# Denser stops, split comparisons and a moved gather in a two-layer graph kernel (quantile aggregation, then message passing) on one core

## The chip, the cores and the metric

The kernel runs on one core of a Trainium2 chip. The metric is the device time of one execution in microseconds (us); lower is better. TensorE is called PE here, its weight loads PEld, VectorE DVE, ScalarE ACT, GpSimd POOL, and SyncE, which issues most of the DMAs, SP.

## The reference, cut to what matters

Sixteen batches of 1,024 nodes with 64 features each, and a symmetric 0/1 adjacency with self-loops, about 16 neighbours to a node. Every node counts as present (`nodemask` is all ones).

```python
# layer 0
nb      = (adj > 0) & ~eye;  m = nb.sum(-1);  rank = cumsum(nb, -1) - 1
skip    = where(m > 10, (m + 1) // 2, 1)
removed = nb & (skip > 1) & ((rank + 1) % skip == 0)
valid   = where(removed | removed.T, 0, adj) > 0          # thinned neighbours, self included
sv      = sort(where(valid, x[None, :, :], big), axis=neighbours)   # for every node and feature
agg     = sum(wt * quantile(sv, tau) for tau, wt in ((.25, .25), (.5, .5), (.75, .25)))
x       = layernorm(x + relu((x + agg) @ W1 + b1) @ W2 + b2)
# layer 1
msg     = adj @ x
x       = layernorm(x + tanh(concat(x, msg) @ W1 + b1) @ W2 + b2)
```

The quantiles interpolate linearly between two places of the sorted list, as is usual. The edge part of layer 1 does not reach the output.

## The kernel before, in words

The 16 batches are treated in nine groups, of 1, 2, 2, 2, 2, 2, 2, 2 and 1 batches. A group goes through these stages, and neighbouring groups overlap.

**Find** (per batch). The adjacency is loaded (`a`, L509, by SP), turned into signs (`nb`, L517), transposed on PE (`nb_t`, L545 and L549), and the neighbours are ranked by products with triangular blocks (`p_rank`, L593 and L596, taken out by ACT as `gone`, L598). What remains is `valid` (L618 to L625). The nodes are sorted by their number of neighbours and put in that order by products with a permutation (`p_srt`, L687 to L691); then DVE reads the neighbours' numbers out of packed words (`codes`, `listed`). The result is `group.index`, the row in `x` of every neighbour of every node.

**Gather**. The sorted nodes of a group make 8·G tiles of 128 nodes (G is 1 or 2), taken in pairs. For every neighbour slot of a tile, POOL issues one indirect DMA (L876) that brings 128 rows of 64 float32 values into the cell `g[:, j]`. Four buffers `g0` to `g3` (`RING = 4`) hold one pair each. A group of two batches has 230 such gathers, its eight pairs 43, 36, 32, 29, 27, 24, 21 and 18; the program has 1,859. Because the nodes are sorted, the first tile has the longest lists. Its slots 24 to 34 are needed by few nodes (the table `FEW`: 23 nodes for slot 24, one for slot 34). In groups 1 to 8 these rare slots are not gathered one by one: 22 small DMAs on SP collect the indices into one column (`few<-index`, L885), ACT fills `few_x` (L886), one indirect DMA on POOL gets all the rows (L887), and 22 DMAs on SP carry them to their cells (`g<-few_x`, L892).

**Sort**. For each node and feature the list is brought into order as far as the quantiles need it, by a network of minima and maxima on DVE: 4,982 `tensor_tensor` instructions on `g` in all, each over 64 to 1,024 elements of a partition. Those of the two tiles of a pair are interleaved. After the last one of a tile, `weigh` lets ACT multiply the needed cells by the quantiles' weights (L907), in place; `add_up` adds them on PE with an identity (`p_agg`, L924 and L928), and ACT takes the sums out as `agg` (L936). A pair's buffer is then free for gathers to come.

**Close** (per batch). The sums go back to the nodes' own order (`p_g`, L965), through the MLP and the layernorm, and layer 1 follows with transposed adjacency blocks (`a_block`, `p_adj` L1135, `adj_t` L1137) and messages (`p_msg`, L1144). For the last groups some of the blocks are transposed ahead (`a_ahead`).

**The order.** The Python code writes the program in an order set by a clock of its own: all DVE instructions pass through the class `Counted`, whose `issue` adds up a modelled time `now` (their line in the profile is L443, whatever they do). `Steps` spreads the steps of find and close over that time: a step is written when its due time has come. The main loop writes the compares of a pair turn by turn, and `around` writes between them what is due. A framework then sets the waits and issues by readiness: the written order is a priority, and each engine's queue runs in order.

**The stops.** In `issue`, ahead of a DVE instruction with two tensor inputs, once `now` has reached `due`, a short one-input reduction is put in (`pause`, L437), which reads two values of the cell written four compares ago; `due` is then set to `GATHER = 1.32` us later. A one-input instruction that passes the due time counts as a stop itself.

```python
if two and self.now >= self.due and len(self.written) >= 4:
    nc.vector.tensor_reduce(pause, self.written[-4], AX.X, ALU.max)
    self.due = self.now + GATHER
```

Of the kernel before, what the change touches and what calls it, by code (L numbers as in the profile page):

```python
# [157 lines left out]
def kernel(  # L158
# [240 lines left out]
    GATHER = 1.32  # L399
# [8 lines left out]
    class Counted:  # L408
# [9 lines left out]
        def __getattr__(self, name):  # L418
# [6 lines left out]
            def issue(out, *args, **more):  # L425
# [10 lines left out]
                if two and self.now >= self.due and len(self.written) >= 4:  # L436
                    nc.vector.tensor_reduce(pause, self.written[-4], AX.X, ALU.max)  # L437
                    self.due = self.now + GATHER
                    self.now += 0.065
                elif not two and self.now + us >= self.due:  # L440
                    self.due = max(self.now, self.due) + GATHER
# [38 lines left out]
    class Group:  # L480


        def __init__(self, number, start, G):
# [3 lines left out]
            self.early = None  # L487
# [343 lines left out]
    def cells(g, box, which, width):  # L831

        start, (d1, n1), (d2, n2) = box
        return bass.AP(tensor=g.tensor, offset=g.offset + start[which] * width,
                       ap=[g.ap[0], [d2[which] * width, n2], [d1[which] * width, n1], [1, width]])
# [15 lines left out]
    def gather(group, at, sorts, lists):  # L851
# [20 lines left out]
        for k, part in zip(pair, parts):  # L872
            u, v = divmod(k, G)
            for j in range(1, min(FEW) if k == 0 and group.number > 0 else TILES[G][k][0]):
                slot_no = first[u] + j - 1
                nc.gpsimd.indirect_dma_start(  # L876
                    out=part[:, j, :], out_offset=None, in_=x_rows,
                    in_offset=bass.IndirectOffsetOnAxis(ap=group.index[:, v, slot_no:slot_no + 1], axis=0),
                    bounds_check=limit, oob_is_err=False)
        if at == 0 and group.number > 0:  # L880
            rows, many = slice(0, G * (P // 2)), lists.tile([P, 1], I32, name="few")
            got = lists.tile([P, C], F32, name="few_x")
            for there, here, j in few(G):
# [3 lines left out]
            nc.gpsimd.indirect_dma_start(  # L887
                out=got[rows], out_offset=None, in_=x_rows,
                in_offset=bass.IndirectOffsetOnAxis(ap=many[rows], axis=0),
                bounds_check=limit, oob_is_err=False)  # L890
            for there, here, j in few(G):
                nc.sync.dma_start(parts[0][here, j], got[there])  # L892
        return parts

    def sort(group, k, g):
# [5 lines left out]
        def compare(op, box):  # L901
            vector.tensor_tensor(cells(g, box, 2, C), cells(g, box, 0, C), cells(g, box, 1, C),
                                    op=op)
            vector.written = vector.written[-3:] + [g[:, box[0][2], :2]]
# [566 lines left out]
```

## Time and profile before

| what | value |
|---|---|
| three runs | 3887.37, 3934.4, 4052.67 us (median 3934.4) |
| the profiled execution | 3815.42 us, span 3813.7 us |
| mean granted TensorE clock in it | 0.709 |
| busy: DVE | 2329.5 us, 61% of the span |
| busy: POOL | 2104.7 us, 55% |
| busy: PE | 1942.5 us, 51% |
| busy: ACT | 1324.3 us, 35% |
| DMA | 205.67 MB, mean 54 GB/s |

The span runs from the first to the last recorded work of the execution; its own device time is 1.7 us longer. A busy share is an average over stages with different limits. In a row of instructions the columns are the line and engine, the operation with output and inputs, the count, the busy time in us and the mean of one in ns, and after the second bar the idle time of the engine just before these instructions, with what ended most of it. "remote" stands for a release that the profile puts down to no engine of this core, "issue" for time in which the engine waited for nothing that the profile shows. SPq is the DMA queue that SP issues to.

### The profile page before, as it was taken

To read this page: it belongs to the slowest core of one execution; us is meant where nothing else is said; L and a number is where in the kernel's file an instruction comes from. 1 tells how busy PE (TensorE), PEld (TensorE's weight loads), DVE (VectorE), ACT (ScalarE), POOL (GpSimd) and SP (SyncE) were. 2 spreads that over 40 slices of the span, in tenths; PEclk is the share of its full clock that TensorE was granted. 3 is DMA by queue.
4 is the path that set the end of the run, shared out by engine and by line. 5 is a ranking of instruction groups with operands and counts; after the bars stand their busy time and mean duration, and the time that the engine had idled before them with its cause. 6 is when DMAs were issued, how large, how long until landed. Compare 5 with 4: busy or idle time off the path is not lost.

```text
span 3813.7 us, 37663 instructions
## 1 busy us (share of the span) xinstructions
PE 1942.5 (51%) x10312; PEld 1070.0 (28%) x10312; DVE 2329.5 (61%) x9225; ACT 1324.3 (35%) x2945; POOL 2104.7 (55%) x1943
## 2 busy tenths in 40 slices
PE   5206523731565442963439635674336645674376
PEld 3103312420333221532224323332113323242133
DVE  4208624991598635885268844877248765768653
ACT  3204423431443332542325323544224334134123
POOL 1760346077654766167572677447571576757750
PEclk9556756765788666875669756786667866777578
DMA  2101111121212201222022212032021321242111
GB/s 99 20 19 48 58 50 32 65 52 24 64 44 87 66 18 62 82 66 43 17 67 93 67 30 65 23 105 64 18 66 28 94 58 26 60 117 62 20 47 29
DMA packets 268306, 205.67 MB, mean 54 GB/s; under 512 B 92634, under 2 KB 225290, under 8 KB 268086
## 3 DMA queue, kind: packets, MB, share of 16 engines
q1 hardware_dynamic: 207382, 147.10, 12.1%
q0 software_dynamic: 59744, 55.90, 7.5%
q8 instruction: 83, 1.36, 0.2%
q14 instruction: 137, 1.12, 0.1%
q10 hardware_dynamic: 960, 0.18, 0.0%
HBM read 203.97 MB, written 4.19 MB: 55 GB/s over the span
## 4 chain that ended last, share of the span: by engine, by line
PE 30%; another core or an unknown queue 25%; DVE 22%; ACT 9%; issue 8%; POOL 4%; DMA 1%; SPq 0%; ACTq 0%; DVEq 0%; POOLq 0%
DVE g L443 12%; PE p_msg L1144 5%; POOL g L876 4%; PE p_srt L687 3%; PE p_g L965 3%; PE p_adj L1135 2%; PE p_rank L596 2%; PE p_rank L593 2%; PE p_agg L924 2%; PE p_cnt L564 1%; PE p_nb L545 1%; ACT nb_t L549 1%; ACT g L907 1%; DVE codes L443 1%
## 5 line engine op out<-in xcount | busy, mean ns | idle before, releaser
L876 POOL DMA_INDIRECT g<-in_x_dram,index x1859 | 2075.7, 1117 | 1470.3 <-issue 560.1
L443 DVE TENSOR_TENSOR g<-g 128x128 f32<-128x128 f32 (+7 forms) x4982 | 1581.3, 373 | 199.7 <-remote 93.7
L545 PE MATMUL p_nb<-ident_h,nb 128*128 128x128 bf16 x1024 | 107.9, 280 | 649.6 <-DVE nb L443 261.9
L437 DVE TENSOR_REDUCE pause<-g 128x1 f32<-128x2 f32 x1021 | 148.5, 145 | 272.2 <-ACT g L907 240.5
L907 ACT ACTIVATE g<-g,weights 128x64 f32<-128x64 f32 x1006 | 260.0, 338 | 102.7 <-DVE g L443 84.3
L965 PE MATMUL p_g<-back,parts 128*64 128x512 bf16 x720 | 197.9, 425 | 186.6 <-DVE back L443 138.5
L443 DVE TENSOR_SCALAR gone<-gone,s 128x1024 bf16<-128x1024 f16 x128 | 64.3, 503 | 362.8 <-ACT gone L598 222.8
L598 ACT ACTIVATE gone<-p_rank,s 128x1024 f16<-128x1024 f32 x128 | 141.5, 1112 | 402.2 <-remote 303.2
L545 PEld LDWEIGHTS <-nb 128*128 128x128 bf16 x1024 | 92.6, 130 | 670.4 <-issue 489.9
L1144 PE MATMUL p_msg<-adj_t,x 128*64 128x512 f32 x416 | 232.3, 661 | 65.9 <-issue 30.4
L593 PE MATMUL p_rank<-after,blocks 8*128 8x512 bf16 x256 | 121.4, 474 | 282.0 <-ACT gone L598 147.5
L549 ACT ACTIVATE nb_t<-p_nb 128x1024 bf16<-128x1024 bf16 x124 | 122.1, 1023 | 375.0 <-remote 247.9
L924 PE MATMUL p_agg<-g,ident 128*128 128x128 f32 x918 | 161.6, 332 | 131.3 <-ACT g L907 83.7
L687 PE MATMUL p_srt<-pay,perm 128*128 128x323 bf16 x1024 | 187.0, 320 | 52.0 <-DVE x_q L443 29.4
L625 ACT ACTIVATE valid<-p_stay 128x1024 bf16<-128x1024 f32 x128 | 130.4, 1019 | 173.5 <-remote 95.0
L924 PEld LDWEIGHTS p_agg<-g,ident 128*128 128x128 f32 x918 | 143.0, 236 | 151.9 <-ACT g L907 96.4
L1137 ACT COPY adj_t<-p_adj 128x512 f32<-128x512 f32 x208 | 117.4, 584 | 162.6 <-PE p_adj L1135 79.0
L596 PEld LDWEIGHTS <-nb_t 128*128 128x128 bf16 x1024 | 70.6, 111 | 365.1 <-issue 365.1
L618 PE MATMUL p_stay<-nb,ident_h 128*128 128x512 bf16 x256 | 115.1, 450 | 105.8 <-ACT valid L625 56.3
L965 PEld LDWEIGHTS <-parts 128*64 128x64 bf16 x720 | 80.0, 119 | 280.1 <-issue 178.8
L517 ACT ACTIVATE nb<-a 128x1024 bf16<-128x1024 f32 x124 | 125.4, 1051 | 67.2 <-remote 27.1
L1135 PE MATMUL p_adj<-ident,a_block 128*128 128x128 f32 x832 | 138.6, 300 | 14.3 <-ACT z_t L1156 11.6
(188 smaller groups left out, 3054.9 us busy)
## 6 DMA issues: line engine op xcount, KB each, us to landing
a<-in_adj_dram SPq DMA_DIRECT2D x64, 1024.0 KB
a_block<-in_adj_dram SPq DMA_DIRECT2D x208, 256.0 KB
g<-in_x_dram,index POOLq DMA_INDIRECT x1859
a_ahead<-in_adj_dram SPq DMA_DIRECT2D x48, 256.0 KB
x_f<-in_x_dram SPq DMA_DIRECT2D x16, 256.0 KB
out_dram<-o SPq DMA_DIRECT2D x16, 256.0 KB
x_c<-in_x_dram SPq DMA_DIRECT2D x15, 256.0 KB
few<-index SPq DMA_DIRECT2D x45, 0.0 KB
```

What stands on the lines that cost most here:

```text
L437: nc.vector.tensor_reduce(pause, self.written[-4], AX.X, ALU.max)
L443: return getattr(nc.vector, name)(out, *args, **more)
L545: nc.tensor.transpose(p[:, t], v["nb"][:, t, block(j)], ident_h)
L549: nc.scalar.activation(v["nb_t"][:, j], p.rearrange("p t c -> p (t c)"), AF.Relu)
L593: nc.tensor.matmul(p[:, half_of(h)], v["blocks"][:, block(t)], after[:, half_of(h)], start=True, stop=False, skip_group_check=True)
L687: nc.tensor.matmul(p[:, k, :PAY], v["perm"][:, t, block(2 * at + k)], pay[:, t], start=(t == 0), stop=False, skip_group_check=True)
L876: nc.gpsimd.indirect_dma_start(out=part[:, j, :], out_offset=None, in_=x_rows, in_offset=bass.IndirectOffsetOnAxis(ap=group.index[:, v, sl ...
L907: nc.scalar.mul(g[:, cell], g[:, cell], group.weights[:, v, u, place:place + 1])
L924: nc.tensor.matmul(p, ident, it, start=(k == 0), stop=(k == most - 1), skip_group_check=True)
L965: nc.tensor.matmul(v["p_g"][h][:C, :HALF], v["parts"][:, k, q], m[:, half_of(h)], start=(k == 0 and v["start"]), stop=(k == 2 and q == v[" ...
L1135: nc.tensor.transpose(p[:, block(t)], m[:, t], ident)
L1144: nc.tensor.matmul(v["p_msg"][C:2 * C, :HALF], v["x1"][:, j, :], adj_t, start=(j == 0), stop=(j == NT - 1))
```

## The change

There are four edits.

1. `GATHER = 1.32` becomes `STOP = 0.44`: the stops are written at least 0.44 us of modelled time apart in place of 1.32. A stop needs only one entry in `written` (before: four), which now keeps eight, as pairs of list and cell; it still reads the fourth-last entry, or the oldest one if there are fewer.
2. `compare` may be cut along its 64 columns. A piece is to end at the due time of the next stop, rounded to an even number of columns; a cut is made only if both pieces have at least `SPLIT = 0.1` us.
3. `weigh` takes the entries of the list that is being weighed out of `written`.
4. The rare slots: the 22 index DMAs and ACT's fill are written ahead of the first tile's gathers, the one indirect DMA behind its 12th slot (`ask`), and the 22 carrying DMAs (`give`) are put off: they are written when the compares of the previous group's last pair begin, or at the latest when their own group's turn comes.

```diff
--- before.py
+++ after.py
@@ -396,7 +396,8 @@
     CLOSING, CLOSING_LAST = 0.8, 60.0
     TURNING = 40.0
     RING = 4
-    GATHER = 1.32
+    STOP = 0.44
+    SPLIT = 0.1
     pause = const.tile([P, 1], F32, name="pause")
 
     def block(t):
@@ -433,12 +434,13 @@
                 us = 0.067 + more_us + n * each
                 two = name in ("tensor_tensor", "tensor_add", "tensor_sub", "tensor_mul",
                                "scalar_tensor_tensor")
-                if two and self.now >= self.due and len(self.written) >= 4:
-                    nc.vector.tensor_reduce(pause, self.written[-4], AX.X, ALU.max)
-                    self.due = self.now + GATHER
+                if two and self.now >= self.due and self.written:
+                    g, cell = self.written[-4:][0]
+                    nc.vector.tensor_reduce(pause, g[:, cell, :2], AX.X, ALU.max)
+                    self.due = self.now + STOP
                     self.now += 0.065
                 elif not two and self.now + us >= self.due:
-                    self.due = max(self.now, self.due) + GATHER
+                    self.due = max(self.now, self.due) + STOP
                 self.now += us
                 return getattr(nc.vector, name)(out, *args, **more)
             return issue
@@ -484,7 +486,7 @@
             self.number, self.start, self.G = number, start, G
             self.x_q, self.node, self.agg = [None] * G, [None] * G, [None] * G
             self.turned = [{} if number >= len(sizes) - 2 else None for _ in range(G)]
-            self.early = None
+            self.early = self.give_few = None
             self.pairs = [(k, k + 1) for k in range(0, NT * G, 2)]
 
         def parts(self, i):
@@ -828,11 +830,12 @@
             to.add(0.2, weigh)
         return to
 
-    def cells(g, box, which, width):
+    def cells(g, box, which, width, columns):
 
         start, (d1, n1), (d2, n2) = box
-        return bass.AP(tensor=g.tensor, offset=g.offset + start[which] * width,
-                       ap=[g.ap[0], [d2[which] * width, n2], [d1[which] * width, n1], [1, width]])
+        return bass.AP(tensor=g.tensor, offset=g.offset + start[which] * width + columns.start,
+                       ap=[g.ap[0], [d2[which] * width, n2], [d1[which] * width, n1],
+                           [1, columns.stop - columns.start]])
 
     def few(G):
 
@@ -869,27 +872,40 @@
                     if which == v:
                         nc.scalar.copy(part[here, 0], group.x_q[i][here, u])
         filled[at % RING] = max(filled[at % RING], start)
-        for k, part in zip(pair, parts):
-            u, v = divmod(k, G)
-            for j in range(1, min(FEW) if k == 0 and group.number > 0 else TILES[G][k][0]):
-                slot_no = first[u] + j - 1
-                nc.gpsimd.indirect_dma_start(
-                    out=part[:, j, :], out_offset=None, in_=x_rows,
-                    in_offset=bass.IndirectOffsetOnAxis(ap=group.index[:, v, slot_no:slot_no + 1], axis=0),
-                    bounds_check=limit, oob_is_err=False)
-        if at == 0 and group.number > 0:
+        rare = at == 0 and group.number > 0
+
+        def few_of_them():
             rows, many = slice(0, G * (P // 2)), lists.tile([P, 1], I32, name="few")
             got = lists.tile([P, C], F32, name="few_x")
             for there, here, j in few(G):
                 slot_no = first[0] + j - 1
                 nc.sync.dma_start(many[there], group.index[here, 0, slot_no:slot_no + 1])
             nc.scalar.copy(got, few_fill.to_broadcast([P, C]))
-            nc.gpsimd.indirect_dma_start(
-                out=got[rows], out_offset=None, in_=x_rows,
-                in_offset=bass.IndirectOffsetOnAxis(ap=many[rows], axis=0),
-                bounds_check=limit, oob_is_err=False)
-            for there, here, j in few(G):
-                nc.sync.dma_start(parts[0][here, j], got[there])
+
+            def ask():
+                nc.gpsimd.indirect_dma_start(
+                    out=got[rows], out_offset=None, in_=x_rows,
+                    in_offset=bass.IndirectOffsetOnAxis(ap=many[rows], axis=0),
+                    bounds_check=limit, oob_is_err=False)
+
+            def give():
+                for there, here, j in few(G):
+                    nc.sync.dma_start(parts[0][here, j], got[there])
+
+            return ask, give
+
+        if rare:
+            ask, group.give_few = few_of_them()
+        for k, part in zip(pair, parts):
+            u, v = divmod(k, G)
+            for j in range(1, min(FEW) if rare and k == 0 else TILES[G][k][0]):
+                slot_no = first[u] + j - 1
+                nc.gpsimd.indirect_dma_start(
+                    out=part[:, j, :], out_offset=None, in_=x_rows,
+                    in_offset=bass.IndirectOffsetOnAxis(ap=group.index[:, v, slot_no:slot_no + 1], axis=0),
+                    bounds_check=limit, oob_is_err=False)
+                if rare and k == 0 and j == min(FEW) // 2:
+                    ask()
         return parts
 
     def sort(group, k, g):
@@ -899,11 +915,21 @@
         todo = []
 
         def compare(op, box):
-            vector.tensor_tensor(cells(g, box, 2, C), cells(g, box, 0, C), cells(g, box, 1, C),
-                                    op=op)
-            vector.written = vector.written[-3:] + [g[:, box[0][2], :2]]
+
+            us = 0.00104 * C * box[1][1] * box[2][1]
+            done = 0
+            while done < C:
+
+                due = vector.due if vector.now < vector.due else vector.now + 0.065 + STOP
+                many = 2 * int(C * (due - vector.now - 0.067) / us / 2 + 0.5)
+                to = C if many * us / C < SPLIT or (C - done - many) * us / C < SPLIT else done + many
+                vector.tensor_tensor(*[cells(g, box, which, C, slice(done, to)) for which in (2, 0, 1)],
+                                     op=op)
+                done = to
+            vector.written = vector.written[-7:] + [(g, box[0][2])]
 
         def weigh(cell, place):
+            vector.written = [w for w in vector.written if w[0] is not g]
             nc.scalar.mul(g[:, cell], g[:, cell], group.weights[:, v, u, place:place + 1])
 
         for op, box in steps:
@@ -1259,11 +1285,19 @@
                 asked[group.number, at] = gather(group, at, sorts, lists)
                 room -= 1
 
+        def give_few(group):
+            if group.give_few:
+                group.give_few()
+                group.give_few = None
+
         for group in groups:
             while group.number not in found:
                 around(group.number - 1, True)
+            give_few(group)
             for at, pair in enumerate(group.pairs):
                 around(group.number)
+                if at == len(group.pairs) - 1 and group is not groups[-1]:
+                    give_few(groups[group.number + 1])
                 lists_of = [sort(group, k, g) for k, g in zip(pair, asked[group.number, at])]
                 turns = sorted(((n + 0.5) / len(l), k, n) for k, (l, _) in enumerate(lists_of)
                                for n in range(len(l)))
```

## The prediction, made before the change was run

> **What bounds the kernel now.** I read the page first, engine totals, then the chain that ended last, then the costliest groups.
>
> ```profile
> PE 1942.5 (51%) x10312; PEld 1070.0 (28%) x10312; DVE 2329.5 (61%) x9225; ACT 1324.3 (35%) x2945; POOL 2104.7 (55%) x1943
> PE 30%; another core or an unknown queue 25%; DVE 22%; ACT 9%; issue 8%; POOL 4%; DMA 1%; SPq 0%; ACTq 0%; DVEq 0%; POOLq 0%
> L876 POOL DMA_INDIRECT g<-in_x_dram,index x1859 | 2075.7, 1117 | 1470.3 <-issue 560.1
> L443 DVE TENSOR_TENSOR g<-g 128x128 f32<-128x128 f32 (+7 forms) x4982 | 1581.3, 373 | 199.7 <-remote 93.7
> L437 DVE TENSOR_REDUCE pause<-g 128x1 f32<-128x2 f32 x1021 | 148.5, 145 | 272.2 <-ACT g L907 240.5
> ```
>
> No engine is full: DVE, the busiest, works 61% of 3813.7 µs. The stages alternate, so a term is worth only what it is worth in its own stage. The change touches three of these rows: the gathers (L876), the compares (L443 on `g`) and the stops (L437, `pause`). The table by 20 µs windows tells where DVE is the limit: in 46 windows DVE is at least 17 µs busy, and they hold 534 of the 1,603 µs of compares and stops, 33%. The chain gives `DVE g` 12% of the span, 446 µs, 28% of the compares. So a microsecond of compares costs about 0.3 µs of span.
>
> **Denser stops, and split compares (DVE's cost).** I applied the diff's rule to the compare lists in written order, with the kernel's own clock. With the old rule this gives 970 to 1,010 stops (the row has 1,021); with the new one 2,679 stops and 5,269 pieces: 1,658 stops and 287 pieces more. The mean interval is 0.61 µs and not 0.44, because a piece that ends just short of the due time gets no stop behind it. The price of one more instruction is in the timeline:
>
> ```profile
> 837.46 1.68 DVE L443 TENSOR_TENSOR g<-g 128x256 f32<-128x256 f32 x5
> 839.06 0.14 DVE L437 TENSOR_REDUCE pause<-g 128x1 f32<-128x2 f32 x1
> 839.13 1.41 DVE L443 TENSOR_TENSOR g<-g 128x256 f32<-128x256 f32 x5
> 838.11 1.90 POOL L876 DMA_INDIRECT g<-in_x_dram,index  x1 [0.30 <-issue]
> ```
>
> The stop lasts 0.14 µs but the next compare begins 0.07 after it: neighbours overlap. A piece costs the same: a 128x64 compare has 216 ns and a 128x512 one 681 ns, 1.04 ns an element, and the start-to-start spacing is 67 ns plus that. Added: 1,658 × 0.065 + 287 × 0.068 = 128 µs of DVE. Here a rule of the Trainium skill speaks against the change: "Advanced Engine Details and Errata", section The Read-Write Bubble, wants tiles of 512 or 1,024 elements since each instruction pays a fixed bubble, and "VectorE: DVE Perf Modes", The TRN2 errata, puts the measured fixed term at about 150 cycles at 0.96 GHz, 156 ns. By that the change would cost 1,945 × 0.156 = 303 µs, a third of it on the path, and the sum below would be −40. The row decides: own times show such a term (145 ns for a stop that reads two elements), but the spacing of 65 to 70 ns is what DVE loses. On the path, 0.3 of 128 is **+40**; 0.28 of it is 36, all of it 128: ends +36 and +128. I take the low one, since the chain and the windows agree on the third.
>
> **Denser stops (POOL's gain).** The gather of the last line starts at 838.11 and ends at 840.01, 0.95 after the stop begins; an undisturbed one lasts 0.99:
>
> ```profile
> L876 POOL DMA_INDIRECT g<-in_x_dram,index x1859: 991/997/4118, 103.7 to 3683.2; - x186
> ```
>
> It was held through the run of compares until the stop. Over all gathers the excess above 0.995 µs is 226 µs, 204 of it under compares and other two-input work. The second rule is "SBUF — State Buffer", section Who interferes with whom: a DVE instruction with two SBUF inputs contends with a reading GpSimd instruction, whoever is first keeps the shared pair for the whole instruction, and tensor_reduce never contends. By that a gather would wait for one compare, 0.68 µs or somewhat more, and denser stops would bring nothing here; the row's maximum of 4.1 µs, 3.1 of it held, shows that a gather waits through several, and the timeline that it goes at the stop. So I go by the row. Replaying the gathers on this timeline with stops every 0.61 µs takes the 226 µs down to about 130. Nearly all of this is hidden: in the middle groups the gathers end long before their compares begin (group 4's first pair gathers from 1773 to 1829 and sorts from 1915). Only at the end, 3123 to 3684, does POOL have little idle left (414 of 561 µs busy, plus 0.3 between gathers); 66 µs of stall lie there, and halving them gives **−30**. Ends: 0, if DVE's order sets that stretch, and −60. By the rule alone this term is 0 and the sum −60.
>
> **The `written` filter in `weigh`.** A stop reads the cell written four compares ago. At the end of a pair that cell is often one which ACT is about to weigh, and DVE waits for ACT:
>
> ```profile
> DVE pause L437 <- ACT g L907: 240.5, 22, 74.1
> 954.36 0.15 DVE L437 TENSOR_REDUCE pause<-g 128x1 f32<-128x2 f32 x1 [74.05 <-ACT g L907]
> 957.76 0.17 DVE L443 COPY s<-p_m 128x8 f32<-128x8 f32 x1 [2.26 <-PE p_m L571]
> 2184.32 0.15 DVE L437 TENSOR_REDUCE pause<-g 128x1 f32<-128x2 f32 x1 [5.44 <-ACT g L907]
> ```
>
> With the entries of the weighed tile gone from `written`, the stop reads the other list of the pair or is left out; the 240.5 µs go. What is late next? The 16 short waits, 2 to 15 µs each, sum 92 µs, lie like the one at 2184.32 before unbroken compares whose rows have long been gathered: DVE is the limit there, so I give back nearly all, **−80** (ends −40 and −92). The six long ones (74, 33, 16, 14, 13 and 11 µs, sum 161 with rounding) lie in stages that find the next batch: after the 74 µs there come three compares, and then `s` waits for PE's `p_m` anyway. PE and ACT are late there, so **−10** (ends 0 and −100, if all that DVE issues later there moved up).
>
> **The rare slots.** Moved are 22 index DMAs on SP, one ACT fill, one POOL gather (to behind the 12th slot) and 22 carrying DMAs on SP, now written at the start of the previous group's last pair or at the group's start. Written order is a priority; readiness decides.
>
> ```profile
> SPq L892 <- remote: 155.3, 4, 48.6
> SPq L509 <- DVE gone L443: 628.8, 9, 188.1
> POOL few_x L887 <- DVE g L443: 70.8, 1, 70.8
> 1758.98 15.24 SPq L892 DMA_DIRECT2D g<-few_x  x22
> ```
>
> Today the carries stop SP's queue in seven of the eight groups that have them, for 18 to 49 µs, until their buffer is free (`p_agg`); behind them stand `x_f`, `x_c`, `out` and the adjacency loads. But the loads `a` wait afterwards for `gone` of DVE, 628.8 µs in all, so an earlier turn helps little. On POOL the rare gather waited 70.8 µs at 736.85, while the next gathers had no buffer until 756; 23.5 at 3368, of which about 8 lie in POOL's full stretch; and 10.6. Each of the eight rare gathers moves past 12 gathers of about 1.3 µs; the carries past nothing needed sooner. I take **−10**; ends −35 (all SP waits that end in a late `x_f`) and, if the carries come to stand behind a blocked load of 1 MB, +15 to +25 in each of seven groups.
>
> **Sum.** +40 −30 −80 −10 −10 = −90. Against the profiled 3815.4 µs that is 3725, ratio 0.976; the profiled execution lies below all three runs shown, so on their median of 3934.4 it is **3840 µs**. About 2% is what a measurement of this kernel can tell from no change; the three runs alone spread over 4%.
>
> **What the sum does not contain.** While gathers stream, ACT and PE are served late, in a way that no operation of the changed code names:
>
> ```profile
> 1801.94 1.02 ACT L549 ACTIVATE nb_t<-p_nb 128x1024 bf16<-128x1024 bf16 x1 [17.20 <-issue]
> 1824.35 1.02 ACT L549 ACTIVATE nb_t<-p_nb 128x1024 bf16<-128x1024 bf16 x1 [21.38 <-remote]
> 1680.00:1720.00 40.00, 28.77 (x116) 14.34 (x113) 39.80 (x156) 18.68 (x48) 31.79 (x27) 0.79 0.31 83
> 1800.00:1840.00 40.00, 5.60 (x24) 2.66 (x24) 0.76 (x2) 4.58 (x6) 22.48 (x23) 0.50 0.09 17
> ```
>
> In the windows (PE, PEld, DVE, ACT, POOL busy, clock, DMA) 1800 to 1840 has 23 gathers, an idle DVE and a PE of 24 matmuls: two `nb_t` steps lie 22.4 µs apart, exactly 1.40 µs for each of the 16 PE instructions between. In 1680 to 1720 with DVE full and 27 gathers PE does 116. Over all streaming windows a done product is taken late by 8.5 µs in 10 when DVE is idle and 1.4 when it is full; among the full ones it falls from 1.75 at 0.3 µs of stall to 0.4–0.7 at 1.5–2.4 µs. So gathers that are held seem to leave PE and ACT room.
>
> **Rivals.**
> - *Slower: the freed gathers delay PE and ACT more.* Place: the sorting stretches in which gathers stream, about 700 µs. Price: +0.6 to +3 µs per 10 µs, so +40 to +200. It decides from +1.3 per 10 µs, where it eats the 90. For it: the rows above. Against: denser stops also pack the same number of gathers into less time, and where POOL idles there is no lateness. At +2.7, +190 − 90 = +100: 3935 + 103 = 4037 µs.
> - *No difference, DVE's cost is on the path.* If stops come every 0.44 (about 3,850) and half of the compares bind, 2,829 × 0.065 + 287 × 0.068 = 203, of which 100 count: 100 − 80 − 10 − 10 + 0 = 0, about 3935. For it: compares are the longest item of DVE; against: the 28 to 33%.
> - *No difference, the carries are late.* +20 in seven groups is +140 against −90: 3815 + 50 = 3865, on the median 3986; with +15 it is +15, 3950. The diff gives them no wait that today's order lacks, so I hold it unlikely.
> - *The rare part does not do what it says.* As readiness places it, the gather may go first as today; then −10 becomes 0, 3850 µs.
> - *Faster still.* The long waits return half of 161 µs: −160, 3770 µs.
>
> **How the numbers follow.** The likeliest case with the two that differ from it by little (ineffective rare part, faster still) has 0.52, mostly under 3856: faster 0.48. DVE's cost and a part of the late carries, 0.23, and the likeliest's upper tail give same 0.27. Slower rival 0.20 and late carries beyond 2% 0.05: slower 0.25. Low: all good ends, +36 −60 −92 −35 −100 = −251, would be 3676, so 3700. High: the slower rival at 4037, so 4040. The likeliest alone: 3770 to 3900.
>
> **What would show it.** Right: `pause` near 2,700 (3,850 at most), `g` compares near 5,270, mean gather down from 1117 to about 1065 ns, `pause <- ACT g` near 0, DVE busy near 2,450 µs, the carries' waits on `remote` gone from SP. Wrong: `pause` waiting for ACT as before (the filter), `gone`, `nb_t` and `agg` with remote waits well above their 303, 248 and 152 µs (the slower rival), DVE's share of the chain above 30% (DVE's cost), a `g` compare that waits for a carry (late carries).

## The result, and the profile after

The changed kernel takes 4101.3 us (median; 4078.4 to 4122.4) beside 3951.7 for the kernel before, a quotient of the medians of 1.038; the ratio is **1.049, 95% interval 1.034 to 1.063**. A ratio here compares only the executions within 1.5% of the fastest of their kernel (two of the four of the kernel before), so it can lie about a per cent above the quotient of the medians, which is given too where it matters. A second comparison (e17_after) gave a ratio of 1.045 (1.040 to 1.050) and a quotient of 1.042. The forecast was 2.4% faster; the change makes the kernel some 4 to 5% slower.

The page of the changed kernel, with the rows that answer to those of before (busy time, then the chain by engine, then the costliest groups):

```profile
PE 1980.0 (48%) x10276; PEld 1079.0 (26%) x10312; DVE 2459.1 (60%) x11318; ACT 1331.1 (32%) x2945; POOL 2054.4 (50%) x1943
DVE 20%; PE 18%; another core or an unknown queue 14%; issue 9%; ACT 5%; DMA 2%; POOL 1%; SPq 0%; DVEq 0%; ACTq 0%; POOLq 0%
L903 POOL DMA_INDIRECT g<-in_x_dram,index x1859 | 2026.9, 1090 | 1646.0 <-issue 597.8
L445 DVE TENSOR_TENSOR g<-g 128x128 f32<-128x128 f32 (+11 forms) x5278 | 1687.9, 359 | 122.2 <-DMA g<-in_x_dram,index 34.0
L439 DVE TENSOR_REDUCE pause<-g 128x1 f32<-128x2 f32 x2818 | 410.6, 146 | 119.3 <-remote 63.7
```

What the change was said to do is there, the gathers' part to about half. There are 2,818 stops (2,679 forecast) and 5,278 pieces (5,269). DVE is busy 130 us longer (128 forecast). The mean gather falls from 1117 to 1090 ns (1065 forecast). No stop waits for ACT any more; the idle time before `pause` is 119 us and not 272. And yet the execution is longer. (The shares of the chain add up to 69%: it was not followed back to the start.)

The first profile of before was of an execution of 3815 us, below every timed run. So the kernel before was profiled once more (e8_again, 3920.6 us), and the traces are compared with that one. Cut at the moments at which the last `index` of groups 2, 3, 4, 7 and 8 (counted from 0) is written, the two kernels stand like this; each line has the stretch, its length, the busy time with counts of PE, PEld, DVE, ACT and POOL, then the granted clock, the busy share of the DMA engines and GB/s. The kernel before:

```profile
721.00:1180.00 459.00, 218.42 (x1207) 124.70 (x1212) 311.12 (x1250) 169.71 (x398) 287.74 (x250) 0.70 0.20 54
1180.00:1618.00 438.00, 233.72 (x1265) 127.22 (x1268) 280.55 (x1110) 162.45 (x369) 243.45 (x221) 0.73 0.21 57
1618.00:3041.00 1423.00, 710.25 (x3846) 386.76 (x3857) 855.54 (x3369) 500.85 (x1126) 754.52 (x693) 0.71 0.21 54
3041.00:3437.00 396.00, 180.37 (x833) 97.10 (x834) 214.07 (x831) 108.71 (x275) 249.13 (x223) 0.66 0.17 37
3437.00:3919.00 482.00, 288.40 (x1141) 154.35 (x1139) 317.56 (x1179) 158.65 (x410) 252.36 (x210) 0.72 0.23 59
```

The changed kernel, same stretches:

```profile
717.00:1271.00 554.00, 240.90 (x1252) 134.10 (x1255) 339.24 (x1559) 167.70 (x395) 263.56 (x248) 0.65 0.16 46
1271.00:1754.00 483.00, 237.84 (x1246) 127.82 (x1252) 297.48 (x1379) 163.54 (x370) 264.53 (x242) 0.71 0.18 52
1754.00:3181.00 1427.00, 726.29 (x3847) 392.69 (x3861) 896.13 (x4162) 504.55 (x1126) 768.14 (x693) 0.72 0.19 54
3181.00:3551.00 370.00, 172.50 (x833) 94.39 (x832) 230.09 (x1040) 108.36 (x273) 227.40 (x204) 0.69 0.15 38
3551.00:4121.00 570.00, 287.30 (x1169) 156.66 (x1169) 350.39 (x1550) 163.28 (x416) 233.22 (x210) 0.70 0.19 51
```

In the three middle groups (third line) DVE has 41 us more work and the length is the same within 4 us: there the cover assumed in the prediction exists. The loss is 95 us in the first stretch (from the `index` of group 2 to that of group 3), 45 in the next one and 88 in the last one; the fourth is 26 us shorter. In each of the two with a large loss DVE's added work (28 and 33 us) is only a third of it. A second profile of the changed kernel (e17_after) repeats the lengths of the first, second, third and last: 545, 480, 1422 and 565 us.

The 20 us windows inside show what fills the rest. The changed kernel, in the middle of the first pair of group 2, whose rows are all there:

```profile
1080.00:1100.00 20.00, 0.00 (x0) 0.00 (x0) 4.26 (x22) 0.38 (x1) 15.34 (x15) 0.53 0.10 24
1100.00:1120.00 20.00, 0.00 (x0) 0.00 (x0) 6.29 (x30) 8.46 (x10) 15.30 (x16) 0.50 0.10 23
1120.00:1140.00 20.00, 0.00 (x0) 0.00 (x0) 4.78 (x15) 0.00 (x0) 13.96 (x14) 0.50 0.10 22
1140.00:1160.00 20.00, 0.00 (x0) 0.00 (x0) 18.40 (x93) 0.00 (x0) 0.00 (x0) 0.50 0.00 0
```

The kernel before (e8_again) in the same stage:

```profile
1040.00:1060.00 20.00, 0.00 (x0) 0.00 (x0) 19.58 (x95) 4.94 (x6) 16.04 (x14) 0.52 0.10 19
1080.00:1100.00 20.00, 19.53 (x134) 9.35 (x132) 19.27 (x78) 11.18 (x14) 16.95 (x11) 1.00 0.22 55
```

While the gathers stream without being held, DVE gets 15 to 30 instructions done in 20 us, PE none; in the window in which the gathers end, DVE does 93. In the kernel before, DVE was full in this stage and nearly as many gathers went on beside it. In the first of these windows DVE waits 16.6 us for `x_q`, which stands behind ACT: PE ends its last product at 1078.9, and ACT, idle from 1082.9 to 1102.5, takes it out at 1103.4. The last stretch holds the same picture from 3820 to 3900 us, where DVE does 68 instructions in 80 us. The timeline there, without most of its gathers:

```profile
3837.47 1.00 POOL L903 DMA_INDIRECT g<-in_x_dram,index  x1 [0.30 <-issue]
3838.77 1.00 POOL L903 DMA_INDIRECT g<-in_x_dram,index  x1 [0.30 <-issue]
3839.80 0.15 DVE L439 TENSOR_REDUCE pause<-g 128x1 f32<-128x2 f32 x1 [3.18 <-issue]
3839.87 0.35 DVE L445 TENSOR_TENSOR g<-g 128x192 f32<-128x192 f32 x1
3841.21 0.96 DVE L445 TENSOR_TENSOR g<-g 128x768 f32<-128x768 f32 x1 [0.99 <-issue]
3842.59 0.15 DVE L439 TENSOR_REDUCE pause<-g 128x1 f32<-128x2 f32 x1 [0.43 <-DVE g L445]
3846.09 0.15 DVE L439 TENSOR_REDUCE pause<-g 128x1 f32<-128x2 f32 x1 [2.48 <-remote]
3848.21 0.15 DVE L439 TENSOR_REDUCE pause<-g 128x1 f32<-128x2 f32 x1 [1.63 <-DVE g L445]
```

A stop lasts 0.15 us but there are 1.4, 2.1 and 3.5 us between the starts of instructions that wait, multiples of about 0.70. What DVE waits for here is its own engine: the semaphore of an earlier instruction of DVE that has already ended. It is the lateness that the prediction had seen on ACT and PE. I added it up from the traces by matching each semaphore wait with the instruction that raises it, and taking the time by which the waiting one starts after both that one's end and its own predecessor's. DVE behind DVE has 204 us in e8_again and 306 in the changed kernel; in the first stretch 16 and 90, in the last one 1 and 78, and in the three middle groups 140 and 27. In the first stretch 28 us of work and 74 of lateness make 102 beside a loss of 95, in the last one 33 and 77 make 110 beside 88.

This fit is no proof. In the middle groups the same sum gives 41 − 113 = −72 where the length changes by +4. Counted over the instructions of DVE that wait for DVE's semaphore alone, the lateness is 189 us in e8_again and 302 in the changed kernel, but also 292 in e3_rare, which is no slower than before, and 327 in e12_nosplit, which is faster than the changed kernel; and e17_after has 39 us in the first stretch and 108 in the last where the first profile has 90 and 78, at nearly the same lengths. So where the loss lies is shown, and that DVE starves there beside streaming gathers; that the late releases make up the loss is argued.

### The profile page after: what moved, and what is told of

Its sections match the earlier page's. It is cut to its first block, busy times and chain, and to the rows that moved or that the text cites. A ratio compares the mean times of both kernels' runs of the same rounds, so it can differ in the third digit from the quotient of the medians.

```text
span 4120.6 us, 39635 instructions
## 1 busy us (share of the span) xinstructions
PE 1980.0 (48%) x10276; PEld 1079.0 (26%) x10312; DVE 2459.1 (60%) x11318; ACT 1331.1 (32%) x2945; POOL 2054.4 (50%) x1943
## 4 chain that ended last, share of the span: by engine, by line
DVE 20%; PE 18%; another core or an unknown queue 14%; issue 9%; ACT 5%; DMA 2%; POOL 1%; SPq 0%; DVEq 0%; ACTq 0%; POOLq 0%
DVE g L445 12%; PE p_msg L1170 4%; PE p_adj L1161 2%; DVE pause L439 2%; PE p_srt L689 2%; PE p_g L991 1%; POOL g L903 1%; PE p_rank L598 1%; PE p_agg L950 1%; PE p_rank L595 1%; ACT g L933 1%; ACT nb_t L551 1%; DVE y L445 1%; DVE ln_st L445 1%
## 5 line engine op out<-in xcount | busy, mean ns | idle before, releaser
L903 POOL DMA_INDIRECT g<-in_x_dram,index x1859 | 2026.9, 1090 | 1646.0 <-issue 597.8
L445 DVE TENSOR_TENSOR g<-g 128x128 f32<-128x128 f32 (+11 forms) x5278 | 1687.9, 359 | 122.2 <-DMA g<-in_x_dram,index 34.0
L439 DVE TENSOR_REDUCE pause<-g 128x1 f32<-128x2 f32 x2818 | 410.6, 146 | 119.3 <-remote 63.7
L595 PE MATMUL p_rank<-after,blocks 8*128 8x512 bf16 x256 | 131.6, 514 | 338.9 <-ACT gone L600 191.6
L620 PE MATMUL p_stay<-nb,ident_h 128*128 128x512 bf16 x236 | 102.8, 435 | 182.2 <-ACT valid L627 90.0
L445 DVE TENSOR_REDUCE x_q<-p_srt 128x128 f32<-128x384 f32 x64 | 35.6, 556 | 238.0 <-ACT srt L693 108.0
```

Of the source, the lines that this page charges most:

```text
L439: nc.vector.tensor_reduce(pause, g[:, cell, :2], AX.X, ALU.max)
L445: return getattr(nc.vector, name)(out, *args, **more)
L595: nc.tensor.matmul(p[:, half_of(h)], v["blocks"][:, block(t)], after[:, half_of(h)], start=True, stop=False, skip_group_check=True)
L903: nc.gpsimd.indirect_dma_start(out=part[:, j, :], out_offset=None, in_=x_rows, in_offset=bass.IndirectOffsetOnAxis(ap=group.index[:, v, sl ...
```

## The experiments

The first twelve and e17_after ran where the kernel before takes 3890 to 4050 us; five others fell into different conditions and stand at the end. The recorded expectations speak of three theories: A, DVE's added time is itself on the path; B, the moved order of the other engines' work costs the time; C, the gathers, held less, slow the other engines (from e13_filler on: DVE too).

### The parts one by one

**Dense stops alone** (e1_stops):

```diff
-    GATHER = 1.32
+    GATHER = 0.44
```

> The kernel before with GATHER = 0.44 in place of 1.32 and nothing else: denser stops, no cuts, no filter, the rare slots as before. Theory (order and cover: the dense stops advance the modelled clock and shift work, and DVE's added time is on the path): slower by 3 to 5%, some 2,000 more stops. Rival (the rare slots' new place holds SP and POOL): no slower than 1.5%. Prediction's sum for this part alone: +10 us.

Measured: 4051.5 us, ratio 1.021 (1.008 to 1.034), with 2,740 stops: about +83 us for 1,719 x 0.065 = 112 us of DVE. The prediction had +40 and −30, together +10.

**The filter alone** (e2_filter):

```diff
-                if two and self.now >= self.due and len(self.written) >= 4:
-                    nc.vector.tensor_reduce(pause, self.written[-4], AX.X, ALU.max)
+                if two and self.now >= self.due and self.written:
+                    g, cell = self.written[-4:][0]
+                    nc.vector.tensor_reduce(pause, g[:, cell, :2], AX.X, ALU.max)
...
         def weigh(cell, place):
+            vector.written = [w for w in vector.written if w[0] is not g]
```

> The kernel before with only the third edit: weigh takes its list out of written, and stops need one entry. Prediction's sum: the 240 us of stops waiting for ACT go and 90 us come back, 2.3% faster. Rival (DVE was not late there, its next work waits for PE and ACT): within 1%.

Measured: 3989.8 us, ratio 1.012 (1.000 to 1.024), quotient of the medians 1.005. The gain of 2.3% is excluded; whether the filter alone costs anything is not. The reason is in DVE's waits. Before (e8_again):

```profile
DVE pause L437 <- ACT g L907: 272.3, 20, 63.3
DVE s L443 <- PE p_m L571: 71.8, 8, 46.4
DVE g L443 <- remote: 54.7, 22, 7.5
DVE d L443 <- remote: 41.7, 5, 12.0
```

With the filter (e2_filter):

```profile
DVE low L444 <- ACT valid L626: 140.5, 8, 35.6
DVE g L444 <- remote: 129.5, 44, 8.0
DVE d L444 <- remote: 122.6, 10, 21.2
DVE s L444 <- PE p_m L572: 117.5, 9, 57.9
DVE back L444 <- remote: 69.6, 7, 14.0
```

The 272 us are gone, and the five rows of the second list, 580 us together, had 199 before; other rows fell (`gone` behind ACT from 270.0 to 190.6). DVE runs into the next waits sooner. Its idle time, span less busy, is 1592 us in e8_again and 1644 here.

**The rare slots alone** (e3_rare; the fourth edit of the change on the kernel before):

```diff
+        if rare:
+            ask, group.give_few = few_of_them()
...
+                if rare and k == 0 and j == min(FEW) // 2:
+                    ask()
```

> The kernel before with only the fourth edit: the rare slots' gather in the middle of its tile and its carries put off. Theory (dense stops are to blame): within 1%. Rival (the moved rare gather holds POOL for its indices, some 35 us in each of the last six groups as in the changed kernel, and SP's queue with it): slower by 3 to 5%.

Measured: ratio 0.995 (0.989 to 1.000); the medians of all executions, 3979.2 of 20 and 3970.4 of 23, have a quotient of 1.002, so this part is not told from no change. The rival falls, although the changed kernel's trace does show the waits that it named:

```profile
POOL few_x L886 <- DMA few<-index: 100.5, 3, 38.1
SPq L882 <- DVE pause L439: 306.2, 5, 94.6
```

POOL waits some 35 us for the indices, but the gathers queued behind have no free buffer yet: in group 5 the rare gather goes at 2246.6 and the next pair's first at 2274.

**The change without the rare slots** (e4_norare; the changed kernel with the old gather):

```diff
-        if rare:
-            ask, group.give_few = few_of_them()
...
+        if at == 0 and group.number > 0:
```

> The changed kernel with the rare slots as before: dense stops, cuts and filter only. Theory (dense stops are to blame): as slow as the changed kernel, 4 to 5% above before. Rival (the rare slots' new place): back to the time before or 1 to 2% below it.

Measured: 4115.5 us, ratio 1.042 (1.032 to 1.053), quotient 1.037. Stops, cuts and filter carry the loss.

**The change without the cuts** (e12_nosplit):

```diff
-    SPLIT = 0.1
+    SPLIT = 99.0
```

> The changed kernel without the cuts (SPLIT = 99): 2,723 stops, 4,982 compares. Theory A: the cuts' 296 x 0.068 = 20 us of DVE go, so 4.2 to 4.5% above before. If the cuts' other effects (gathers released at shorter intervals) matter, it lies outside of 3.5 to 5%.

Measured: 4066.5 us, ratio 1.028 (1.018 to 1.038), beside 1.045 (1.040 to 1.050) for the whole change in e17_after. Some 296 cuts, and 95 stops that come with them, cost about 1.7%, 65 us (the two intervals allow 0.6 to 2.8%), where their DVE time is some 26 us. Why so much is open: without the cuts DVE's lateness behind itself is no smaller (327 us, above).

### Is it DVE's time, the order, or the freed gathers?

**Dense stops in the old order** (e5_uncounted; the modelled clock counts only the stops of the old rule) and **the new order with the old stops** (e6_order; it counts the dense ones but issues one every 1.32 us):

```diff
-                if two and self.now >= self.due and len(self.written) >= 4:
+                if two and self.now >= min(self.due, self.dense) and len(self.written) >= 4:
                     nc.vector.tensor_reduce(pause, self.written[-4], AX.X, ALU.max)
-                    self.due = self.now + GATHER
-                    self.now += 0.065
+                    self.dense = self.now + STOP
+                    if self.now >= self.due:
+                        self.due = self.now + GATHER
+                        self.now += 0.065
...
```

> Dense stops (0.44 us apart, 2,851 of them) in the kernel before, but the modelled clock counts only those that the old rule would write, so the order of the other work stays near the old one (326 of ACT's 2,792 instructions stand elsewhere, with plain dense stops 1,955). Theory A (the dense stops' own DVE time is on the path): as slow as e1_stops, 2% above before. Theory B (the shifted order of ACT's, PE's and SP's work costs it): within 0.7%. Theory C (gathers that are held less slow PE and ACT): 2% slower.

```diff
-    GATHER = 1.32
+    GATHER = 0.44
+    BEFORE = 1.32
...
+                    if self.now >= self.counted:
+                        nc.vector.tensor_reduce(pause, self.written[-4], AX.X, ALU.max)
+                        self.counted = self.now + BEFORE
...
```

> The modelled clock counts dense stops (0.065 us every 0.44 us), but a stop is issued only at the old spacing: 1,006 stops, with the written order of the dense kernel nearly (of the 1,955 ACT instructions that plain dense stops move, most move here too: 1,831 in all). No DVE work is added and gathers are held as before. Theories A and C: within 0.7% of before. Theory B: 2% slower, like e1_stops.

Measured: e5_uncounted 1.026 (1.013 to 1.040), e6_order 1.014 (1.003 to 1.024); the quotients of the medians are 1.019 and 1.002. The stops cost about as much in the old order; so the order isn't needed for the loss. What it adds by itself is between nothing and 2%.

**Each stop three times** (e7_triple):

```diff
-                    nc.vector.tensor_reduce(pause, self.written[-4], AX.X, ALU.max)
+                    for _ in range(3):
+                        nc.vector.tensor_reduce(pause, self.written[-4], AX.X, ALU.max)
```

> Each stop of the kernel before is issued three times in a row at the old spacing: 3,063 in all, 2,042 x 0.065 = 133 us more of DVE, no denser releases of the gathers, order near the old one. Theory A: the 133 us come in at 60 to 80%, as the 112 us of e1_stops did, 2 to 2.7% slower. The prediction's third of it: 1.0%. Theories B and C: within 0.7%.

Measured: 1.031 (1.020 to 1.042), +121 us for 133 of DVE (by the medians +75). It was meant to leave the gathers' releases alone and did not: the framework put compares between the three (in the trace only 4 stops follow directly on another), and the mean gather fell to 1087 ns. So it speaks for a cost of the stops and does not decide between A and C.

**The kernel before again** (e8_again):

> The kernel before, unchanged, for a second profile: the first one is of an execution of 3815 us, below every other run of it. If the first was an unusually fast execution, this one has 3900 to 4000 us, and its late releases to ACT and DVE (the remote waits) are longer by some 100 us in sum.

It is the trace used above. ACT starts late behind finished PE work by 1094 us in sum, 1043 in the first profile: less of a difference than expected.

**Stops where DVE is idle, and where it is full** (e9_low, e10_full):

```diff
...
+                vector.times = 9 if group.G == 2 and at >= 5 else 1           # e9_low
+                vector.times = 5 if group.G == 2 and 1 <= at <= 4 else 1      # e10_full
```

> The kernel before with every stop issued nine times while the last three pairs of a two-batch group are compared, where DVE is 15 to 35% busy in most windows: 1,656 more stops, 108 us, order near the old one. The prediction's step (only full DVE stretches count): within 0.5%, since DVE has the room. Theory A (DVE's queue runs in order, so added time stands before the small DVE steps of find and close everywhere): slower by 1.7 to 2.7%, 65 to 105 us.

> The same with five of each stop while pairs 1 to 4 of a two-batch group are compared, where DVE is 60 to 100% busy: 1,804 more stops, 117 us. The prediction's step and theory A both: slower by 2 to 3%. If this is near nothing and e9_low is slow, both are wrong.

Measured: e9_low 1.024 (1.016 to 1.033), e10_full 1.051 (1.043 to 1.059). This is the test of the third. Where DVE is mostly idle, 108 us of stops cost about 97 us (by the medians 59) and not nothing; where it is full, 117 us cost about 200 (by the medians 168), more than they last. DVE's late releases behind itself are 594 and 583 us in these two, 204 in e8_again.

**Fewer stops** (e11_few_stops):

```diff
-    GATHER = 1.32
+    GATHER = 4.0
```

> The kernel before with GATHER = 4.0: 365 stops in place of 1,021, 43 us less of DVE, gathers held longer. Theory A: 0.7 to 1% faster. The prediction's stall term (gathers held longer delay POOL's full stretch): slower by 1 to 3%. Theory C (held gathers leave PE and ACT room): faster by more than 1%.

Measured: 1.034 (1.023 to 1.045). Theories A and C both fall as simple rules: 43 us less of DVE and gathers held longer make the kernel slower. The prediction's stall term, 1 to 3%, comes nearest. The gathers' excess above 0.995 us grows from 209 us in e8_again to 354:

```profile
L876 POOL DMA_INDIRECT g<-in_x_dram,index x1859 | 2203.5, 1185 | 1512.4 <-issue 595.2
L443 DVE TENSOR_TENSOR g<-g 128x128 f32<-128x128 f32 (+7 forms) x4982 | 1547.0, 370 | 283.8 <-DMA g<-in_x_dram,index 128.1
```

The compares now wait 128 us for rows. Of the three spacings tried in the kernel before, the old 1.32 is the best here.

### Where releases are prompt

Five runs (e13 to e16, e18) fell into conditions in which the kernel before takes 3019 to 3021 us. The kernel is the same; what differs is that hardly anything is released late: ACT behind PE 33 to 42 us in sum and DVE behind DVE 1, where it was about 1100 and 200. What sets these conditions no trace shows. They go with the chip that was used: every execution on record from chips 2, 5, 7 and 11 is in the late conditions and every one from chips 10 and 12 in the prompt ones, but each experiment ran on one chip only, so that chip and time are not told apart.

**DVE time that holds the gathers** (e13_filler, and e18_filler2, the same kernel once more):

```diff
...
-                    nc.vector.tensor_reduce(pause, self.written[-4], AX.X, ALU.max)
+                    nc.vector.tensor_reduce(pause, self.written[-4][:, :2], AX.X, ALU.max)
+                    nc.vector.tensor_tensor(both, self.written[-4], self.written[-4], op=ALU.max)
...
```

> The kernel before with a two-input maximum over 64 elements behind each of its 1,021 stops (result unused): 1,021 x 0.134 = 137 us more of DVE, in instructions that hold the gathers as compares do; no denser releases; order near the old one. Theory A (DVE's time is on the path): 2 to 3% slower, as with 1,700 to 2,000 more stops. Theory C (more stops let the gathers stream without a break, and while they stream every release, DVE's own too, comes late): within 1%.

> The kernel before with a two-input maximum over 64 elements behind each of its 1,021 stops, as in e13_filler: 137 us more of DVE, no further stops. e13_filler fell into conditions in which releases are prompt and before takes 3021 us; its 3.4% there can be the gathers, held longer (1229 ns each). Here it is wanted where before takes 3950 us and releases are late. Theory A (DVE's own time is on the path): 2 to 3.5% slower. Theory C (freed gathers make releases late): within 1%.

Measured: 1.034 (1.031 to 1.038) and 1.035 (1.032 to 1.038). They don't decide between A and C, since no release is late here to begin with; the mean gather is 1229 ns.

**Gathers set apart** (e14_spaced on the kernel before, e15_after_spaced on the changed one):

```diff
...
                     bounds_check=limit, oob_is_err=False)
+                nc.gpsimd.memset(space, 0.0)
```

> The kernel before with a memset of 128x128 on POOL behind each gather, about 0.2 us each, 1,859 of them: POOL has 370 us more, the gathers start 1.5 us apart and not 1.3; nothing else is moved. Theory C: late releases to ACT and PE fall clearly (1,043 to 1,094 us of ACT behind PE before), and the time by 1 to 4%. Theory A: no gain, 0 to 3% slower since POOL's full stretch at the end grows.

> The changed kernel with the same memset behind each gather. Theory C: DVE's waits for its own earlier instructions in the last stretch and between the second and third group's index (78 and 90 us of 306) go, and the time comes back to 0 to 2% above before. Theory A: 4 to 6% above before, as the changed kernel or more.

Measured: 1.118 (1.114 to 1.123) and 1.107 (1.102 to 1.111). 1,859 memsets of 0.211 us are 392 us of POOL, and the kernel before grows by 352 by the medians: in these conditions POOL's stream of gathers is the path. With it stretched, the changed kernel is 1.1% faster than the kernel before (1.107 / 1.118 = 0.990).

**Dense stops in groups 2 to 6 only** (e16_ends, on the changed kernel):

```diff
+            vector.apart = STOP if 2 <= group.number < 7 else 1.32
...
-                    self.due = self.now + STOP
+                    self.due = self.now + self.apart
...
```

> The changed kernel with stops 0.44 us apart for groups 2 to 6 only, and 1.32 us for groups 0, 1, 7 and 8: 2,149 stops. Where the two traces are compared by stretch, the middle groups (their period is 475 us in both) take the dense stops without loss. Theory from the stretches: the loss of about 85 us in the last stretch and a part of the 100 us between the second and third index go, so 1 to 2.5% above before. If each stop costs the same everywhere: 669 of 1,797 stops fewer, 3 to 3.5%.

Measured: 2996.4 us, ratio **0.992 (0.991 to 0.994)**, faster than the kernel before. Its page:

```profile
DVE 28%; PE 25%; POOL 24%; issue 9%; DMA 7%; ACT 5%; SPq 1%; ACTq 0%; DVEq 0%; POOLq 0%
L904 POOL DMA_INDIRECT g<-in_x_dram,index x1859 | 2175.7, 1170 | 682.7 <-issue 519.8
L440 DVE TENSOR_REDUCE pause<-g 128x1 f32<-128x2 f32 x2149 | 308.0, 143 | 0.0
```

In e8_again the chain reads

```profile
PE 27%; DVE 26%; another core or an unknown queue 24%; issue 10%; ACT 8%; DMA 2%; POOL 2%; SPq 1%; DVEq 0%; ACTq 0%; POOLq 0%
```

"Another core or an unknown queue" has gone from it in e16_ends, and POOL has 24%. In a window of this run in which 15 gathers stream unheld, PE does 141 matmuls and DVE 89 instructions:

```profile
1690.00:1710.00 20.00, 18.45 (x141) 11.55 (x141) 17.29 (x89) 17.35 (x46) 15.74 (x15) 0.97 0.26 69
```

So PE and DVE can work while gathers stream; from 1120 to 1140 above, with 14 gathers, PE did nothing and DVE 15 instructions. A low count alone is no sign of a late release, though: in the same run PE does nothing and DVE 27 instructions from 1740 to 1760, because DVE waits 26.0 us for rows. With 1,128 more stops and some 280 more pieces than before, 92 us of DVE, this variant (which also has the filter and the moved rare slots) is 0.8% faster all the same. The expectation for the late conditions stays untested for this kernel.

**The changed kernel once more** (e17_after):

> The changed kernel itself, once more. In the last four runs the kernel before took 3021 us, not 3970, and next to nothing of ACT's, PE's and DVE's work was released late (some 30 us in all, 1,300 before). If this run has such conditions: gathers are then the path in the middle groups (period 340 to 355 us for 230 gathers), dense stops free them, and the changed kernel is 0 to 2% faster than before; if DVE's own time were what costs, it would be 2 to 4% slower, like e13_filler. If this run has the conditions of the first twelve: 4 to 5.5% slower, as it was.

Measured: 4120.9 us, ratio 1.045 (1.040 to 1.050), in the late conditions. The changed kernel itself was not run in the prompt ones.

## Why the prediction was wrong

- **Counts and prices: right.** Stops, pieces and the added DVE time came within a few per cent of the forecast, and a compare starts 65 ns after a stop (median of 2,699 in the changed kernel). DVE is busy 130 us longer and not 303, so the row was the right choice against the 156 ns of the Trainium skill ("VectorE: DVE Perf Modes", The TRN2 errata), the figure from which the 303 were estimated.
- **A third of DVE's time on the path: wrong, and the first step that failed.** It was +40. With the −30 for the gathers the stops were to cost +10; e1_stops shows about +83. One of the two readings behind the third was itself wrong: over the whole span 67 windows of 20 us, not 46, have DVE at least 17 us busy, and they hold 920 of the 1,603 us, 57%, which would have made +73. And the share was an average over the span. By stretch the cost is nothing in the middle groups and three times the added work in the two stretches that lengthen most; e9_low shows that idle windows are not free, and e10_full that full ones cost more than the time added.
- **The filter: the second step that failed, and the largest.** The waits went as forecast, but instead of −90 came +47 (0 to +95; by the medians +19). The step took "unbroken compares follow" for "DVE is the limit"; DVE met the next late product sooner (rows of e2_filter).
- **The gathers' stall:** the excess fell from 226 to 177 us and not to 130, and the −30 in the last stretch did not come; that stretch is 88 us longer.
- **The cuts:** put at 287 x 0.068 with a third of it, 6 us; about 65 in e12_nosplit beside e17_after.
- **The rare slots: not refuted.** −10, with an end at −35; e3_rare gives −21 (−42 to −1) by the ratio and +9 by the medians, so the size is not shown.
- Stops 2.1, filter 1.2, cuts 1.7 and rare slots −0.5 make 4.5%, the measured ratio. Each part is uncertain by about a per cent, except the rare slots by half of one, so the exact match is luck.
- **The rival "the freed gathers delay PE and ACT more"** put the loss on late releases and came nearest with 4037 us, but had the wrong engines: ACT behind PE fell from 1094 to 894 us, while DVE behind DVE rose from 204 to 306. That it is the freeing of the gathers which brings DVE into these stretches was not shown: e11_few_stops frees them less and is slower too, and in its last stretch DVE is busy for about 30 of the 100 us from 3829 to 3929 while gathers stream.

What stays open: why releases come late on four chips and not on two; how much of the loss the late releases make up; what starts a stretch in which DVE starves beside streaming gathers; and whether DVE time without more stops would cost the same in the late conditions, since both runs of the filler fell into the prompt ones.

## What to carry to other kernels

A share of the chain, or of busy windows, is no price for added work. In the late conditions 1,656 to 2,042 added stops cost, by the ratios, 97 to 200 us for 108 to 133 us of DVE (e7, e9, e10), where the third would have made about 40: add the work in one stage at a time (as e9_low and e10_full do) or compare the two traces by stretches that end at the same event. A wait that is taken away only pays if the next wait on that engine does not end at the same time; look up that wait before a gain is booked. And a fit of one term, like DVE's lateness in two stretches here, has to be tried on a stretch and a run that did not get slower.

## What the runs showed that was not expected

- An engine's own earlier result can reach it late: in the timeline above DVE starts 0.4 to 3.2 us after it last ended, with nothing but its own earlier work to wait for. In the first stretch it did 15 to 30 instructions in 20 us while 14 to 16 gathers streamed, and 93 in the window in which they ended.
- The same kernel took 3887 to 4053 us in most runs and 3001 to 3033 in others, and an edit that costs 4.5% in the former gains about 1% in the latter in a close variant (e16_ends; e15_after_spaced against e14_spaced).
- Stops written in a row don't stay in a row: the framework put other work between all but 4 of the tripled ones.
